# A selective scan laid out as four state groups over whole images, with its front spread behind it and a part of its products moved to POOL

## The chip, the cores and the metric

One core of a Trainium2 chip runs the whole network in one launch. The metric is the time of that launch on the device, in microseconds. Every kernel below ran at least four times on the same chip as the kernel before. The rounds ran on several chips; the median of the kernel before was 11377 to 11384 us on each, so runs of different rounds are compared here too. All the runs of one kernel agree within 0.3%.

## The reference

Four layers follow one another on a batch of 8 images. The first two hold a Mamba block: a norm, an input projection, a causal convolution with four taps, silu, a selective scan with 16 states for each of 768 channels, a gate and an output projection. Between and after them come an attention pooling, an MLP, two depthwise convolutions of 13 x 13 and a pointwise one. The change touches only the two Mamba blocks:

```python
u = silu(conv1d(xin))                       # 768 channels, 1024 tokens an image
dbc = u @ x_proj_w.T                        # step ranks, B and C
delta = softplus(dt_lo @ dt_proj_w.T + dt_proj_b)
def step(h, inp):
    dt_t, u_t, B_t, C_t = inp
    dA = exp(dt_t[..., None] * A)           # A: 768 x 16
    h = h * dA + (dt_t * u_t)[..., None] * B_t[:, None, :]
    y = einsum('bdn,bn->bd', h, C_t)
    return h, y
out = ((y + u * D) * silu(z)) @ out_proj_w.T
```

## The kernel before

Channels lie on the partitions, 6 chunks of 128. An image is two units of 512 tokens. For one chunk, ACT writes the decay (an exponential) into PSUM, POOL multiplies B by du, DVE scans and multiplies by C, and PE adds the 16 states up with an identity matrix. In the middle of a unit the next unit's front (norm, projection, convolution, silu) is issued.

```python
def softplus(s, d):
    ...                                                   # one product on PE into ps
    nc.scalar.activation(e, ps, AF.Abs, bias=dt_b[:, d : d + 1])
    nc.vector.tensor_scalar(delta, ps, dt_b[:, d : d + 1], 0.0, ALU.add, ALU.max)
    nc.scalar.activation(e, e, AF.Exp, scale=-1.0)
    nc.scalar.activation(r, e, AF.Identity, bias=k["one"])
    nc.scalar.activation(lw, e, AF.Ln, bias=k["one"])
    nc.vector.scalar_tensor_tensor(r, r, 1.0, e, ALU.subtract, ALU.subtract)
    nc.vector.tensor_tensor(lw, lw, r, ALU.subtract)
    nc.vector.tensor_tensor(delta, delta, lw, ALU.add)

def scan(s, d, y):
    delta = softplus(s, d)
    du = work.tile([P, T], F32, tag="du", name="du")
    nc.vector.tensor_tensor(du, delta, u, ALU.mult)
    for j in range(NS // 2):                              # two states at a time
        nc.gpsimd.tensor_tensor(dbu, s["Bt"][j], du.unsqueeze(1).to_broadcast([P, 2, T]), ALU.mult)
        for q in range(2):
            nc.scalar.activation(h[:, q], delta, AF.Exp, scale=A[:, n : n + 1])     # h in PSUM
        for q in range(2):
            nc.vector.tensor_tensor_scan(h[:, q], h[:, q], dbu[:, q], first, ALU.mult, ALU.add)
        if half == 0:
            nc.vector.tensor_copy(state[:, d, 2 * j : 2 * j + 2], h[:, :, T - 1])
        nc.vector.tensor_tensor(hc, h, s["Ct"][j], ALU.mult)
        for q in range(2):
            nc.tensor.matmul(acc, k["ident"], hc[:, q], ...)
    ...                                                   # y = (u * D + acc) * gate

for i in range(NU):
    gates(s, range(KD // 2))
    exp_ln()                                              # the table set of exp and ln
    for d in range(KD // 2):
        scan(s, d, y)
    gates(s, range(KD // 2, KD))
    nxt = front(i + 1) if i + 1 < NU else None
    exp_ln()
    for d in range(KD // 2, KD):
        scan(s, d, y)
    ...
```

In each queue the instructions stand in one order, which is fixed when the program is built. The building step puts the instructions in order by the dependencies, by the program order and by estimated durations.

## Time and profile before

| | before |
|---|---|
| time (median) | 11379 us |
| first layer, from the start to its last output | 4152 us |
| one image in the steady part of a layer | 515 us |
| of it DVE busy / idle | 450 / 62 us |
| from the start of the layer to its first scan | 77 and 63 us |
| stretches that the change does not touch | 3078 us |

DVE is the fullest engine of the layers, and its share falls below six tenths only outside them. Idle time is the sum of DVE's gaps over 0.15 us. I also use a third number below, "blocked": for each instruction of DVE, its duration above the tenth percentile of the instructions of the same line and shape, added up. It measures how long DVE stands inside an instruction without progress. In the kernel before it is 21 us an image.

### The profile page before, as it was taken

Reading aid. Unit: us, or ns where it says so; the run is one execution under the profiler, and the core shown is the slowest. Engines: PE = TensorE matmul, PEld = TensorE weight load, DVE = VectorE, ACT = ScalarE, POOL = GpSimd, SP = SyncE. Lnnn points to the kernel's source line nnn. Section 1 sums busy time; section 2 is a strip of 40 time slices with the busy share of each in tenths; the row PEclk is TensorE's granted clock in tenths of the full one; section 3 lists DMA queues with packets and bytes.
Section 4 is the critical chain, followed back from the end, with each engine's and each line's share of the span. In section 5 each row is a group of like instructions: output and inputs, shape, how many; then the busy total and the mean of one; then the engine's idle time right before and its main releaser. Section 6 shows DMA issues by size and latency. Waiting matters only on the chain. (4 is left out here: it accounts for less than half of the span.)

```text
span 11377.1 us, 62759 instructions
## 1 busy us (share of the span) xinstructions
PE 8400.4 (74%) x18924; PEld 3687.4 (32%) x18924; DVE 7542.9 (66%) x8579; ACT 4328.4 (38%) x6060; POOL 3877.4 (34%) x1750
## 2 busy tenths in 40 slices
PE   6676677767677665766767677666676888889999
PEld 2222222222222211222222222222222333358688
DVE  7888888888888863788888888888887111110100
ACT  4444444444444432444444444444443221210100
POOL 3444444444444430344444444444444000001011
PEclk8898989888888886889888988888888999989999
DMA  1111111111111100111111111111110101024444
GB/s 62 60 44 38 41 38 38 39 38 38 56 55 38 36 29 28 54 44 62 44 38 41 38 38 39 38 38 47 59 41 29 22 17 22 15 55 84 128 85 79
DMA packets 703234, 523.10 MB, mean 46 GB/s; under 512 B 553344, under 2 KB 566784, under 8 KB 701872
## 3 DMA queue, kind: packets, MB, share of 16 engines
q1 hardware_dynamic: 573616, 456.16, 13.7%
q10 hardware_dynamic: 120064, 37.76, 1.3%
q0 software_dynamic: 9216, 25.18, 1.0%
q8 instruction: 150, 2.46, 0.1%
q14 instruction: 188, 1.54, 0.0%
HBM read 438.81 MB, written 80.15 MB: 46 GB/s over the span
## 5 line engine op out<-in xcount | busy, mean ns | idle before, releaser
L218 POOL TENSOR_TENSOR dbu<-Bt,du 128x1024 f32<-128x1024 f32 x1536 | 3683.4, 2403 | 5037.6 <-DVE h L226 2493.6
L232 PE MATMUL acc<-hc,ident 128*128 128x512 f32 x6144 | 3476.6, 701 | 2045.0 <-DVE hc L230 2032.7
L222 ACT ACTIVATE h<-delta,A 128x512 f32<-128x512 f32 x3072 | 2095.6, 689 | 3074.2 <-DVE hc L230 3030.7
L232 PEld LDWEIGHTS acc<-hc,ident 128*128 128x128 f32 x6144 | 1236.2, 218 | 4260.8 <-DVE hc L230 3168.8
L226 DVE TENSOR_TENSOR_SCAN h<-h,state,dbu 128x512 f32<-128x512 f32 x1536 | 1920.7, 1276 | 108.5 <-POOL dbu L218 101.6
L226 DVE TENSOR_TENSOR_SCAN h<-h,dbu 128x512 f32<-128x512 f32 x1536 | 1842.1, 1218 | 114.7 <-POOL dbu L218 106.0
L230 DVE TENSOR_TENSOR hc<-h,Ct 128x1024 f32<-128x1024 f32 x1536 | 1854.5, 1211 | 14.7
L433 PE MATMUL ps<-xp,wt 128*128 128x256 f32 x4992 | 1100.2, 382 | 20.0 <-DMA wt<-k_cols 20.0
L433 PEld LDWEIGHTS ps<-xp,wt 128*128 128x128 f32 x4992 | 942.5, 189 | 178.0 <-issue 21.0
L370 DVE SCALAR_TENSOR_TENSOR x<-ps_fc,vecs,x 128x512 f32<-128x512 f32 x48 | 36.0, 750 | 1019.3 <-PE ps_fc L369 1019.3
L182 PE MATMUL ps_z<-xt,w_in 128*128 128x512 f32 x1152 | 617.0, 679 | 88.2 <-ACT zs L187 44.3
L246 PE MATMUL ps_out<-y,w_out 128*128 128x512 f32 x1152 | 596.2, 654 | 106.2 <-DVE y L236 67.7
L364 PE MATMUL ps_fc<-xt,fc 128*128 128x512 f32 x1152 | 533.9, 627 | 126.8 <-ACT xt L93 126.8
L428 POOL DMA_DIRECT2D xp<-x x192 | 169.8, 885 | 1302.6 <-PE ps L433 910.9
L135 PE MATMUL ps_in<-xt,w_in 128*128 128x512 f32 x1152 | 550.0, 619 | 47.8 <-ACT xt L93 47.8
L369 PE MATMUL ps_fc<-h,fc 128*128 128x512 f32 x1152 | 497.0, 592 | 0.0
L435 ACT ACTIVATE o<-ps,b_grp 128x256 f32<-128x256 f32 x192 | 91.1, 475 | 1002.8 <-PE ps L433 1002.8
L473 DVE TENSOR_TENSOR o<-o,xt 128x512 f32<-128x512 f32 x48 | 33.3, 693 | 655.2 <-ACT o L470 655.2
L152 DVE SCALAR_TENSOR_TENSOR u<-xp,vecs,u 128x512 f32<-128x512 f32 x576 | 422.0, 744 | 4.2
L85 ACT ACTIVATE sq<-xt 128x512 f32<-128x512 f32 x192 | 113.8, 624 | 807.7 <-DVE xt L81 759.4
L357 POOL COPY xt<-x 128x1536 f32<-128x1536 f32 x16 | 23.5, 1469 | 1133.4 <-PE ps_fc L364 1095.0
L182 PEld LDWEIGHTS ps_z<-xt,w_in 128*128 128x128 f32 x1152 | 237.7, 214 | 448.4 <-issue 298.7
(124 smaller groups left out, 6390.7 us busy)
## 6 DMA issues: line engine op xcount, KB each, us to landing
Bt<-bc SPq DMA_DIRECT2D x256, 512.0 KB, 4.3
Ct<-bc SPq DMA_DIRECT2D x256, 512.0 KB, 4.8
wt<-k_cols SPq DMA_DIRECT2D x768, 52.0 KB, 2.7
xt<-x SPq DMA_DIRECT2D x48, 768.0 KB, 5.1
x<-o SPq DMA_DIRECT2D x96, 256.0 KB, 2.0
xp<-x POOLq DMA_DIRECT2D x192, 128.0 KB, 4.3
xt<-in_x_dram SPq DMA_DIRECT2D x16, 768.0 KB, 4.4
o<-in_x_dram SPq DMA_DIRECT2D x48, 256.0 KB, 2.8
```

The lines of the kernel that those rows point to most:

```text
L135: nc.tensor.matmul(ps, w_in[:, c, d * P : (d + 1) * P], xt[:, c], start=c == 0, stop=c == KC - 1)
L152: nc.vector.scalar_tensor_tensor(u, xp[:, j : j + T], conv_w[:, 4 * d + j : 4 * d + j + 1], u, ALU.mult, ALU.add)
L182: nc.tensor.matmul(ps, w_in[:, c, DI + d * P : DI + (d + 1) * P], s["xt"][:, c], start=c == 0, stop=c == KC - 1)
L218: nc.gpsimd.tensor_tensor(dbu, s["Bt"][j], du.unsqueeze(1).to_broadcast([P, 2, T]), ALU.mult)
L222: nc.scalar.activation(h[:, q], delta, AF.Exp, scale=A[:, n : n + 1])
L226: nc.vector.tensor_tensor_scan(h[:, q], h[:, q], dbu[:, q], first, ALU.mult, ALU.add)
L230: nc.vector.tensor_tensor(hc, h, s["Ct"][j], ALU.mult)
L232: nc.tensor.matmul(acc, k["ident"], hc[:, q], start=j == 0 and q == 0, stop=j == NS // 2 - 1 and q == 1)
L246: nc.tensor.matmul(ps, w_out[:, d, m * P : (m + 1) * P], y[:, d], start=d == 0, stop=d == KD - 1)
L364: nc.tensor.matmul(ps, w1[:, c, m * P : (m + 1) * P], xt[:, c], start=c == 0, stop=c == KC - 1)
L369: nc.tensor.matmul(ps, w2[:, f, m * P : (m + 1) * P], h[:, f], start=f == 0, stop=f == KF - 1)
L433: nc.tensor.matmul(ps, wt[:, j], xp[:, :, j : j + HW], start=j == 0, stop=j == KS - 1)
```

## The change

The intent is to take load off DVE and to make its instructions longer. A block is 32 channels by four groups of states on the 128 partitions, so that one scan goes over 1024 tokens and no state is carried between halves. The sum over the four groups is a product with a 128x32 matrix that writes 32 rows of PSUM, a different group of the array's columns for each block. Of eight products with C, three go to POOL, with the scan writing SBUF for these. Silu runs in bursts of six, with an added order on ACT: all earlier activations first, then the burst, then the rest. The front of the next image and the output of the last are spread over the scan in 48 slots. Delta, du, u, z and y travel through memory to change their layout. The first tap of the convolution and the max in softplus go from DVE to ACT.

```diff
+POOL_C = (2, 5, 7)
...
-                u = work.tile([P, T], F32, tag="u", name="u", bufs=9)
-                nc.vector.tensor_scalar(
-                    u, xp[:, 0:T], conv_w[:, 4 * d : 4 * d + 1], conv_b[:, d : d + 1], ALU.mult, ALU.add
-                )
+                    nc.scalar.activation(
+                        u, xp[:, 0:T], AF.Identity, bias=conv_b[:, d : d + 1], scale=conv_w[:, 4 * d : 4 * d + 1]
+                    )
...
+                act.burst([(z, z, AF.Silu) for z in zs])
+                for d in range(KD):
+                    nc.sync.dma_start(s["uz"][d][:, 1, cols], zs[d])
+                yield
...
-            nc.vector.tensor_scalar(delta, ps, dt_b[:, d : d + 1], 0.0, ALU.add, ALU.max)
+            nc.scalar.activation(delta, ps, AF.Relu, bias=dt_b[:, d : d + 1])
...
+                for q in range(4):
+                    nc.sync.dma_start(t[32 * q : 32 * q + 32], s["dd"][d][32 * j : 32 * j + 32, i])
...
+                            w_ = work.tile([P, L], F32, tag="slab", name="slab", bufs=6)
+                            nc.gpsimd.tensor_tensor(w_, s["Bt"][n], du4, ALU.mult)
+                            h = ps_da.tile([P, L], F32, tag="h", name="h")
+                            nc.scalar.activation(h, dl, AF.Exp, scale=A[:, at : at + 1])
+                            if (2 * n + i) % 8 in POOL_C:
+                                nc.vector.tensor_tensor_scan(w_, h, w_, 0.0, ALU.mult, ALU.add)
+                                nc.gpsimd.tensor_tensor(w_, w_, s["Ct"][n], ALU.mult)
+                            else:
+                                nc.vector.tensor_tensor_scan(h, h, w_, 0.0, ALU.mult, ALU.add)
+                                nc.vector.tensor_tensor(w_, h, s["Ct"][n], ALU.mult)
+                            hs.append(w_)
+                        for half in range(2):
+                            for i in range(2):
+                                rows = slice(32 * (2 * jp + i), 32 * (2 * jp + i) + 32)
+                                nc.tensor.matmul(
+                                    acc[rows, half], k["sel"], hs[i][:, half * T : (half + 1) * T],
+                                    start=n == 0, stop=n == NL - 1,
+                                )
+                        pull()                            # one slot of the front behind
...
```

## The prediction

> **What bounds the kernel now.** I read the page first (busy shares, slices, costliest groups), then a table of stretches.
>
> ```profile
> PE 8400.4 (74%) x18924; PEld 3687.4 (32%) x18924; DVE 7542.9 (66%) x8579; ACT 4328.4 (38%) x6060; POOL 3877.4 (34%) x1750
> ...
> DVE  7888888888888863788888888888887111110100
> ACT  4444444444444432444444444444443221210100
> POOL 3444444444444430344444444444444000001011
> ...
> L218 POOL TENSOR_TENSOR dbu<-Bt,du 128x1024 f32<-128x1024 f32 x1536 | 3683.4, 2403 | 5037.6 <-DVE h L226 2493.6
> ...
> L226 DVE TENSOR_TENSOR_SCAN h<-h,state,dbu 128x512 f32<-128x512 f32 x1536 | 1920.7, 1276 | 108.5 <-POOL dbu L218 101.6
> L226 DVE TENSOR_TENSOR_SCAN h<-h,dbu 128x512 f32<-128x512 f32 x1536 | 1842.1, 1218 | 114.7 <-POOL dbu L218 106.0
> L230 DVE TENSOR_TENSOR hc<-h,Ct 128x1024 f32<-128x1024 f32 x1536 | 1854.5, 1211 | 14.7
> ```
>
> The two plateaus of DVE at 8 tenths are the two scan layers. PE has the largest share of the span, but much of it lies in the tail, where DVE is nearly empty. In the layers POOL is at 4 tenths and waits for DVE's scans, which barely wait for POOL (some 0.1 ms per row). Three rows, two forms of the scan and the product with C, hold 5617 us of DVE. The next view is three stretches: one steady image of the second layer (two units of 512 tokens), then the pooling between the layers and everything after the second layer.
>
> ```profile
> 5171.70:5689.00 517.30, 361.48 (x672) 132.07 (x672) 450.88 (x504) 240.82 (x333) 230.41 (x98) 0.88 0.13 42
> ...
> 4151.00:4594.00 443.00, 247.52 (x393) 80.52 (x393) 142.18 (x235) 108.99 (x168) 0.00 (x0) 0.69 0.11 38
> 8742.00:11377.00 2635.00, 2371.08 (x7780) 1493.58 (x7780) 192.41 (x277) 418.49 (x625) 193.35 (x208) 0.94 0.28 58
> ```
>
> After the length come PE, PEld, DVE, ACT and POOL busy. In an image DVE works 450.9 of 517.3 us and idles 66. The change does not touch the last two stretches: 443 + 2635 = 3078 us stay. The two layers are the other 8299 us, 4150 each, and the whole change has to earn its money there. The chain of waits is of no use: it names the depthwise convolutions, which merely come last.
>
> **The lock between DVE and POOL.** POOL is to get more work, so I asked what the two do to each other. Two neighbouring steps of softplus, both reading two SBUF tiles, and then the timeline around one late product:
>
> ```profile
> L206 DVE TENSOR_TENSOR sp_l<-sp_l,sp_r x192: 665/692/2227, 71.9 to 8649.7; 128x512 f32<-128x512 f32 x192
> ```
> ```profile
> L207 DVE TENSOR_TENSOR delta<-delta,sp_l x192: 666/674/694, 72.6 to 8667.8; 128x512 f32<-128x512 f32 x192
> ```
> ```profile
> 4013.49 2.35 POOL L218 TENSOR_TENSOR dbu<-Bt,du 128x1024 f32<-128x1024 f32 x1 [2.39 <-DVE h L226]
> ...
> 4015.03 1.36 DVE L236 TENSOR_TENSOR y<-y,zs 128x512 f32<-128x512 f32 x1
> ```
>
> Same shape, same engine: L206 goes up to 2227 ns, L207 never above 694. I matched each with POOL's products in the trace: 50 of the 192 L206 begin while POOL is running, with 1409 ns of it left, and take 1956 ns on average; the other 142 take 678. No L207 begins under a POOL product. In the timeline L236 begins at 4015.03, POOL ends at 4015.84, DVE at 4016.39: 0.81 us waiting, 0.55 us working. The scans (1166 begin under POOL, mean 1248 ns, against 1246 of the rest) are not touched; they read one tile from PSUM and one from SBUF.
>
> **What the Trainium skill says.** "SBUF — State Buffer", section "Who interferes with whom": a DVE instruction with two SBUF inputs and a GpSimd instruction that reads SBUF exclude one another for a whole instruction; with at most one SBUF input there is no contention. The figures above agree. "GPSIMD Engine Reference", section "Elementwise — side-by-side cycle accounting": a two-input product costs POOL about 2.6 cycles an element at 1.2 GHz, DVE about one at 0.96 GHz; for 1024 elements that is 2.2 us against 1.1 us, and the rows show 2.40 (2.35 undisturbed) and 1.21. So moving a product saves DVE 1.2 us and costs POOL 2.35. "ScalarE: Activation LUTs", section "What ACT_TABLE_LOAD costs": 1283 ns a load, the duration that this trace has for every load. "TensorEngine Tiling (Array Packing)", section "Key Properties": tiles can run in parallel; no run here shows it yet.
>
> **The change part by part, one image.** Elements to scan: 24 blocks x 4 states x 1024 = 98304 columns, as before (6 x 16 x 1024). Putting four state groups on the partitions therefore saves no scan work, only instruction starts and the state copies.
>
> Scan, 96 of 128x1024. A tensor_tensor takes 680 ns for 512 columns (L207) and 1211 for 1024 (L230): about 149 ns fixed. Taking the same off 1247 leaves 1098 ns per 512 columns, so 2 x 1098 + 149 = 2.345 us each; 225.1 us. Before: 192 x 1.247 = 239.4.
> Product with C: 96 x 1.211 = 116.3 before; 5 of 8 stay, 60 x 1.211 = 72.7. The other 36 go to POOL.
> Removed: state copies (48 x 0.15 = 7.2; they came in one half only, so 3.6 a unit), first tap of the convolution (12 x 0.537 = 6.4) and softplus's max (12 x 0.738 = 8.9), both to ACT.
> Kept front, by its rows without blocking: taps 36 x 0.744 = 26.8; softplus and du 48 x 0.68 = 32.6; norm 2 x 6 = 12; carries 3.
> Output: 12 x 0.737 + 6 x 1.21 = 16.1 for y; 6 x 0.75 = 4.5 for the residual.
> Sum 392.8 us of durations. Neighbours overlap: in the steady unit durations of 242 make 225 us of union over 264 instructions, 0.063 us each; with some 290 instructions that is 18. DVE works about 374 us an image, 77 less than now.
>
> POOL: 96 + 36 = 132 products x 2.35 = 310 us, from 230. In about 460 us it is 67% full before any blocking, from 45%.
>
> Lock: DVE instructions with two SBUF inputs are 36 taps, 48 of softplus and du, 6 of the norm and 6 for y: 96. Today few meet POOL (L207, du and the taps never do, in step with the scan). With the front spread behind the scan and POOL two thirds full I take 55% of them to meet it, with 1.3 us left (1.28 and 1.41 us in today's L205 and L206): 96 x 0.55 x 1.3 = 69 us. This is where I chose, and it is the largest uncertainty.
>
> Other idle time of DVE: today 66 us an image, mostly waiting for ACT in the norm and softplus, with no scan in the queue at that place. Scan work now stands between, and of the loads of tables only 8 an image remain, in four bursts of 6 x 0.63 + 2 x 1.28 = 6.3 us, which two exponentials ahead (some 7 us of scan and products) nearly hide. I leave 20 us.
>
> Image with a front behind it: 374 + 69 + 20 = 463 us, against 515.
>
> Beside it: ACT has 96 exponentials of about 1.15 us (the 8x1024 exponential of the pooling took 1147 ns) and perhaps 110 us of the rest, half the time. PE has as many instructions as now, 361 us. Transfers: dl and du4 24 x 1 MB, B and C 4 MB, u, z, y out and in and delta, du out 25 MB, x and the result 5 MB: 58 MB, 125 GB/s; the third slice from the end of today's page moves 128 GB/s with the DMA engines 4 tenths busy. Loads are issued two blocks ahead, some 35 us, where today's land in 2 to 5 us.
>
> Ends of a layer: the first scan starts at 76.9 us now, after half an image's front. A whole image, with gates, softplus and a trip through memory, is 170 us by estimate. The last image has no front behind it: 225 + 73 + 16 + 4.5 less overlap is 307, POOL 310; 330. Its output projection, halves in turn from memory, is 45.
> Layer: 170 + 7 x 463 + 330 + 45 = 3786, against 4150. Total 2 x 3786 + 3078 = 10650 us, 6.4% faster.
>
> **Rivals.** (1) The lock takes the gain. Consecutive taps may let POOL in between each, so that each waits a whole 2.35 us; at 0.9 x 1.8 x 96 = 156 us the image takes 550 and the total about 11900. L205's 1834 ns under POOL speaks for it; against it, POOL is then itself delayed and has idle time left, and a waiting tap works as soon as POOL ends. (2) POOL bounds the quiet stretches: two slots need 2.75 x 2.35 = 6.5 us of POOL, 6.1 of DVE. With only six slabs nothing averages over longer stretches. That costs 10 to 20 us an image, total 10900. (3) The queue of transfers or the fixed order on ACT starves the scan: some 310 issues an image at 0.4 us are 125 us, but a store whose data are late holds the loads behind it; 11200 if it happens at each step. (4) The lock costs little, because the order of the queues falls into step as it does today (25 us), and idling nearly vanishes: 410 an image, 9900.
>
> **Range and chances.** Between (4) and part of (1) to (3): 10050 to 11150, eight times in ten. Faster by over 2% (below 11151) 0.88; within 2% 0.08; slower 0.04.
>
> **What would show it.** Scan of 1024 columns at 2.3 to 2.4 us; DVE busy, waits within it included, 440 to 460 us an image; taps and softplus above 1.1 us in the mean, with maxima above 2.2 us; POOL near 70% in the layers; steady image 463 us; the stretches outside the layers unchanged. Wrong if the scan's row has kept 2.5 us, if DVE idles over 60 us an image on POOL, ACT or transfers, or if the two-input rows stay at 0.7 us (then the time is near 9700, the sum without the 69 us).

## The result and the profile after

The changed kernel takes 11953 us (median of 4, 11945 to 11954), the kernel before 11379. The ratio is 1.050 (95% interval 1.049 to 1.052): slower by 5%, where 6.4% faster was predicted. Ratios here are the mean time of one kernel's runs over that of the other's of the same rounds, so they are not quite the ratios of the medians.

The page of the changed kernel: busy shares, slices, and the groups that answer to those of before. After the bar stand busy us and mean ns, then the idle time of the engine before the group.

```profile
PE 7955.7 (67%) x18924; PEld 2948.1 (25%) x18924; DVE 7085.9 (59%) x5222; ACT 3809.7 (32%) x4718; POOL 5442.1 (46%) x2326
...
DVE  4878787777777773388777787877878110110000
...
POOL 2656565565655670066655565655668000001011
...
L271 POOL TENSOR_TENSOR slab<-Bt,du 128x1024 f32<-128x1024 f32 x1536 | 3819.1, 2513 | 2409.2 <-DMA dl<-dd 1005.2
L279 DVE TENSOR_TENSOR_SCAN h<-h,slab 128x1024 f32<-128x1024 f32 x960 | 2184.9, 2286 | 1252.0 <-ACT h L274 730.7
...
L277 POOL TENSOR_TENSOR slab<-slab,Ct 128x1024 f32<-128x1024 f32 x576 | 1450.5, 2518 | 1615.0 <-DVE slab L276 1467.5
...
L276 DVE TENSOR_TENSOR_SCAN slab<-h,slab 128x1024 f32<-128x1024 f32 x576 | 1310.1, 2274 | 19.9 <-ACT h L274 12.5
L280 DVE TENSOR_TENSOR slab<-h,Ct 128x1024 f32<-128x1024 f32 x960 | 1151.4, 1208 | 10.4 <-DVE h L279 0.5
...
L188 DVE SCALAR_TENSOR_TENSOR u<-xp,vecs,u 128x512 f32<-128x512 f32 x576 | 728.1, 1276 | 67.7 <-ACT u L184 67.7
```

DVE's work fell, from 7543 to 7086 us, and POOL's rose, from 3877 to 5442. In a steady image no engine is as full as DVE was (450 of 515 us; now DVE works 425 of 556). But the main scan now has 1252 us of idle time ahead of it, where the two rows of before had 223 between them, and a tap of the convolution (L188) went from 744 to 1276 ns though nothing in it was changed. The tap's row in the kernel before was:

```profile
L152 DVE SCALAR_TENSOR_TENSOR u<-xp,vecs,u 128x512 f32<-128x512 f32 x576 | 422.0, 744 | 4.2
```

A steady image of the changed kernel, then the two stretches that should not have moved (length, then busy PE, PEld, DVE, ACT, POOL):

```profile
2391.40:2947.30 555.90, 331.32 (x672) 85.32 (x672) 425.72 (x294) 201.21 (x243) 329.36 (x132) 0.75 0.37 107
...
4462.00:4905.00 443.00, 248.26 (x393) 80.91 (x394) 142.20 (x235) 109.52 (x168) 0.00 (x0) 0.69 0.11 38
9316.00:11951.00 2635.00, 2373.46 (x7780) 1494.27 (x7780) 192.38 (x277) 418.20 (x625) 193.10 (x208) 0.94 0.28 58
```

The untouched stretches are 3078 us again, to within 1 us. Everything happened in the two layers. From the times of the first scan of each image in both traces, the 574 us of profile span divide like this:

| | before | after | difference, both layers |
|---|---|---|---|
| start of a layer to its first scan | 77, 63 | 224, 211 | +295 |
| seven images of a layer, each | 516 | 546 | +423 |
| last image and the rest of the layer | 469, 469 | 402, 393 | -143 |

The last image is shorter because nothing of a front runs behind it. For DVE the sums below are means over the third to seventh image of the first layer, in us an image:

| | before | after |
|---|---|---|
| time | 515 | 556 |
| DVE busy | 450 | 425 |
| of it blocked | 21 | 64 |
| DVE idle | 62 | 129 |

So 68 us of work are gone (450 - 21 against 425 - 64), blocking took back 43 and idling 68, and the image is 41 us longer.

Where is the idle time? Four places recur in each image. First, twice an image, at the gates of the two halves (the timeline of the changed kernel; start, duration, and in brackets the idle time before it):

```profile
2492.93 1.12 ACT L274 ACTIVATE h<-dl,A 128x1024 f32<-128x1024 f32 x1 [0.87 <-DVE slab L276]
2504.36 2.23 ACT L96 ACTIVATE xt<-xt,vecs 128x512 f32<-128x512 f32 x3 [10.31 <-DVE xt L91]
2509.13 0.58 ACT L156 COPY z<-ps_z 128x512 f32<-128x512 f32 x1 [2.54 <-PE ps_z L149]
...
2523.90 3.23 ACT L404 ACTIVATE z<-z 128x512 f32<-128x512 f32 x6
2527.14 1.28 ACT L395 ACT_TABLE_LOAD   x1
2528.44 2.15 ACT L274 ACTIVATE h<-dl,A 128x1024 f32<-128x1024 f32 x2
...
2500.55 3.78 DVE L91 TENSOR_TENSOR xt<-xt,rs_y 128x1536 f32<-128x1536 f32 x1
2529.65 4.48 DVE L279 TENSOR_TENSOR_SCAN h<-h,slab 128x1024 f32<-128x1024 f32 x2 [25.33 <-ACT h L274]
```

ACT is idle most of the time between 2493 and 2524, but the next exponential of the scan stands behind the burst in its queue, the burst behind six copies of z, these behind the projection on PE and that behind the norm on DVE. The end of the norm, L91, itself takes 3.78 us, twice its usual 1.75, because it waits first for a product of POOL that ends at 2502.71. DVE then has nothing to scan for 25 us.

Second, at each start of an image (SPq is the queue that issues the loads):

```profile
2915.51 1.36 SPq L237 DMA_DIRECT2D Bt<-bc  x3
2925.97 0.34 SPq L296 DMA_DIRECT2D y<-uzt  x1
2926.41 2.14 SPq L237 DMA_DIRECT2D Bt<-bc  x4
2928.60 7.84 SPq L237 DMA_DIRECT2D Ct<-bc  x16
2936.73 1.88 SPq L248 DMA_DIRECT2D dl<-dd  x4
2938.84 1.91 SPq L248 DMA_DIRECT2D du<-dd  x4
...
2924.72 1.23 DVE L295 TENSOR_TENSOR uzt<-uzt 128x1024 f32<-128x1024 f32 x1
2947.35 2.30 DVE L279 TENSOR_TENSOR_SCAN h<-h,slab 128x1024 f32<-128x1024 f32 x1 [21.40 <-POOL slab L271]
```

The queue stands 9.0 us, from 2916.9, at the store of y (L296), because DVE finishes the last sum of the image (L295) only at 2925.95. The loads of B and C stand behind this store, although the last use of the old C ended at 2919.7; from the third image of a layer on, each starts with the same 9 us. Then a load starts every 0.5 us or so, and twenty of them are ten us before dl and du even start. Third, the output of the image before, whose 36 records stand in one piece in PE's queue, ahead of the sums of the scan:

```profile
2424.78 17.34 PE L309 MATMUL ps_out<-yt,w_out 128*128 128x512 f32 x36
...
2442.06 5.34 PE L285 MATMUL acc<-slab,sel 128*32 128x512 f32 x22
```

During these 17 us PE frees no slab (a buffer of a product). This first time it costs little: POOL then idles 1.9 us for a slab and DVE 2.2 us for POOL's product. The second half of the output, 17.03 us from 2452.66, costs more: DVE stands 4.4 us at the output itself and then 11.4 us at the sum that PE has not reached. Fourth, DVE's own collection of a finished sum waits at the head of DVE's queue, 32 us an image in six pieces, of which those 11.4 us are one.

The blocking is visible in the two-input instructions. These are rows of softplus in the changed kernel (minimum, median, maximum), to be held against L206 and L207 of the prediction:

```profile
L226 DVE TENSOR_TENSOR sp_l<-sp_l,sp_r x192: 656/679/2836, 87.7 to 8884.3; 128x512 f32<-128x512 f32 x192
```
```profile
L227 DVE TENSOR_TENSOR delta<-delta,sp_l x192: 658/668/2718, 88.4 to 8887.0; 128x512 f32<-128x512 f32 x192
```

The step that never met a POOL product before (694 ns at most) now goes up to 2718.

### The profile page after: what moved, and what is told of

Same layout as the page of the kernel before. It is cut to its first block, busy times and chain, and to the rows that moved or that the text cites. A ratio compares the mean times of both kernels' runs of the same rounds, so it can differ in the third digit from the quotient of the medians.

```text
span 11950.9 us, 65751 instructions
## 1 busy us (share of the span) xinstructions
PE 7955.7 (67%) x18924; PEld 2948.1 (25%) x18924; DVE 7085.9 (59%) x5222; ACT 3809.7 (32%) x4718; POOL 5442.1 (46%) x2326
## 4 chain that ended last, share of the span: by engine, by line
PE 29%; DVE 14%; issue 8%; POOL 6%; DMA 3%; ACT 3%; SPq 0%; DVEq 0%; POOLq 0%; ACTq 0%
PE ps L575 9%; PE ps_fc L506 4%; PE ps_fc L511 4%; POOL slab L271 4%; DVE h L279 4%; PE ps_z L149 2%; POOL slab L277 2%; PE ps_out L309 2%; DVE u L188 2%; PE acc L285 2%; DVE slab L276 2%; DVE slab L280 1%; PE var L89 1%; PE ps L611 1%; PE mean L83 1%
## 5 line engine op out<-in xcount | busy, mean ns | idle before, releaser
L285 PE MATMUL acc<-slab,sel 128*32 128x512 f32 x6144 | 2963.4, 851 | 3010.2 <-DVE slab L280 1715.6
L271 POOL TENSOR_TENSOR slab<-Bt,du 128x1024 f32<-128x1024 f32 x1536 | 3819.1, 2513 | 2409.2 <-DMA dl<-dd 1005.2
L279 DVE TENSOR_TENSOR_SCAN h<-h,slab 128x1024 f32<-128x1024 f32 x960 | 2184.9, 2286 | 1252.0 <-ACT h L274 730.7
L274 ACT ACTIVATE h<-dl,A 128x1024 f32<-128x1024 f32 x1536 | 1709.2, 1116 | 3478.5 <-DVE slab L280 1674.2
L277 POOL TENSOR_TENSOR slab<-slab,Ct 128x1024 f32<-128x1024 f32 x576 | 1450.5, 2518 | 1615.0 <-DVE slab L276 1467.5
L285 PEld LDWEIGHTS acc<-slab,sel 128*32 128x32 f32 x6144 | 478.4, 132 | 5377.9 <-POOL slab L277 1843.3
L276 DVE TENSOR_TENSOR_SCAN slab<-h,slab 128x1024 f32<-128x1024 f32 x576 | 1310.1, 2274 | 19.9 <-ACT h L274 12.5
L280 DVE TENSOR_TENSOR slab<-h,Ct 128x1024 f32<-128x1024 f32 x960 | 1151.4, 1208 | 10.4 <-DVE h L279 0.5
L188 DVE SCALAR_TENSOR_TENSOR u<-xp,vecs,u 128x512 f32<-128x512 f32 x576 | 728.1, 1276 | 67.7 <-ACT u L184 67.7
L309 PE MATMUL ps_out<-yt,w_out 128*128 128x512 f32 x1152 | 544.5, 632 | 25.1 <-DMA yt<-y 23.6
```

Of the source, the lines that this page charges most:

```text
L188: nc.vector.scalar_tensor_tensor(u, xp[:, j : j + T], conv_w[:, 4 * d + j : 4 * d + j + 1], u, ALU.mult, ALU.add)
L271: nc.gpsimd.tensor_tensor(w_, s["Bt"][n], du4, ALU.mult)
L274: nc.scalar.activation(h, dl, AF.Exp, scale=A[:, at : at + 1])
L276: nc.vector.tensor_tensor_scan(w_, h, w_, 0.0, ALU.mult, ALU.add)
L277: nc.gpsimd.tensor_tensor(w_, w_, s["Ct"][n], ALU.mult)
L279: nc.vector.tensor_tensor_scan(h, h, w_, 0.0, ALU.mult, ALU.add)
```

## The experiments

Two theories were to be told apart. "Order": the pace is set by instructions that wait at the head of an in-order queue while others behind them could run. "Lock": the pace is set by DVE and POOL excluding one another, that is, by the products moved to POOL. Later a third appeared, "work": waits only show where an engine's work binds, so that removing one makes another.

All runs in one table; time is the median, the ratio is to the kernel before, the other columns are as above (us an image, mean of five images of the first layer). The second layer differs from the first by up to 10 us an image in most of these kernels, and by more in e14 (502 against 485) and e16 (484 against 495); a difference of a few us in one layer alone is therefore weak evidence. The record's verdict, which needs 2%, is "same" for e8, e10, e11 and e12 and "unclear" for e9, but the intervals of all five exclude a ratio of 1.

| run | time | ratio | image | DVE busy | of it blocked | idle |
|---|---|---|---|---|---|---|
| before | 11379 | 1 | 515 | 450 | 21 | 62 |
| after | 11953 | 1.050 | 556 | 425 | 64 | 129 |
| e1_late | 11808 | 1.038 | 543 | 424 | 61 | 117 |
| e2_onedma | 11890 | 1.045 | 532 | 419 | 58 | 112 |
| e3_no_pool_c | 12060 | 1.060 | 564 | 458 | 55 | 105 |
| e4_taps_psum | 11791 | 1.036 | 542 | 410 | 48 | 131 |
| e5_no_order | 11856 | 1.042 | 546 | 431 | 67 | 112 |
| e7_evict | 11870 | 1.043 | 549 | 425 | 63 | 122 |
| e8_all | 11493 | 1.010 | 502 | 403 | 42 | 98 |
| e9_no_pool | 11159 | 0.980 | 493 | 406 | 3 | 85 |
| e6_before_pool_c | 12047 | 1.059 | 556 | 446 | 54 | 106 |
| e10_before_pool_c2 | 11443 | 1.005 | 519 | 433 | 44 | 83 |
| e11_before_act | 11513 | 1.011 | 524 | 440 | 24 | 80 |
| e12_before_both | 11480 | 1.009 | 522 | 427 | 52 | 90 |
| e13_before_ahead | 10876 | 0.956 | 485 | 455 | 29 | 27 |
| e14_ahead_pool_c | 11024 | 0.969 | 485 | 448 | 66 | 35 |
| e15_ahead_act | 10778 | 0.947 | 474 | 446 | 31 | 25 |
| e16_ahead_both | 10981 | 0.965 | 495 | 444 | 72 | 47 |

### Removing one wait from the changed kernel

**e1_late**, the gates' burst three slots later in program order:

```diff
-                act.burst([(z, z, AF.Silu) for z in zs])
-                for d in range(KD):
-                    nc.sync.dma_start(s["uz"][d][:, 1, cols], zs[d])
                 ...
                 for d in range(KD):                      # the convolution
+                    if d == 3:
+                        act.burst([(z, z, AF.Silu) for z in zs])
+                        ...                              # and the stores of z; one more buffer of u and z
```

> The gates' silu burst comes three slots later in program order. Theory 'order' (scan starves behind the fixed order on ACT): the two waits of some 25 us an image of the scan for its exponential vanish, an image falls from 551 to about 505 us, the total to about 11250. Theory 'lock' (DVE and POOL excluding each other set the pace): the waits shrink but the scan then runs into POOL; less than 200 us in all, above 11750.

The wait for the exponential fell from 53 to 11 us an image, but the image only from 556 to 543: DVE's wait for POOL's slabs rose from 35 to 45, softplus got 8 and the carry 4 of its own. That is 145 us in all. "Lock" was nearer in its number; what the time went to, though, was mostly new waits (blocking even fell by 4).

**e5_no_order**, the silus without the added order on ACT:

```diff
     def burst(self, todo):
+        for out, x, func in todo:
+            self.nc.scalar.activation(out, x, func)
+        return
         before = self.close()
```

> Silu activations without the added order on ACT; the schedule may put exponentials between them, with more loads of tables. Theory 'order': the 53 us an image of the scan waiting for its exponential fall below 20, ACT gains perhaps 50 us of table loads an image, which it has free; image 515 to 530, total 11400 to 11600. If ACT's loads then hold the scan instead: above 11900.

Near e1: the wait for exponentials fell to 27 us (20 in one scan's row and 6 in the other), ACT worked 264 us an image in place of 201 because of the table loads, and the image got 11 us shorter. The strict order on ACT is thus a cause of the long waits, but not the whole of the loss; my 11400 to 11600 was missed.

**e2_onedma**, one transfer of 128 partitions where there were four of 32:

```diff
-                for q in range(4):
-                    nc.sync.dma_start(t[32 * q : 32 * q + 32], s["dd"][d][32 * j : 32 * j + 32, i])
+                nc.sync.dma_start(t, s["dd"][d][32 * j : 32 * j + 32, i].unsqueeze(0).to_broadcast([4, 32, L]))
```

(and B and C likewise)

> B, C, dl and du4 each loaded by one transfer over 128 partitions in place of four over 32. Theory 'order': the wait of 22 us at each start of an image, which is 36 issues of 0.48 us one after the other, falls to about 8, and loads held up behind the output's get shorter: 15 to 25 us an image, total 11600 to 11750. Theory 'lock': no change beyond 100 us.

A steady image lost 25 us, as "order" said; DVE's wait for POOL's slabs fell from 35 to 3. The total fell by 63 us only. The trace shows where the rest went: the last image and what follows grew from 402 to 491 us, because the building step had now put the collection of a sum earlier in DVE's queue there, and DVE stood 15 us at it four times. One edit far away reordered another stretch.

**e7_evict**, the collection after the next chunk's first two scans in program order:

```diff
                             hs.append(w_)
+                        if acc is None:
+                            if last is not None:
+                                finish(s, *last)         # collects the chunk before
+                            acc = ps_y.tile([P, 2, T], F32, tag="acc", name="acc")
+                            ...                          # and the load of u and z for this chunk
```

> The changed kernel with the collection of a finished chunk's sum put after the first two scans of the next chunk in program order. Theory 'order': DVE's wait for the sum, 32 us an image, falls below 10 and an image to about 530, total about 11600. If the wait merely moves to POOL's slabs: above 11850.

A miss. The wait fell only from 32 to 28 us an image; program order did not change much in the order of the queue. The image is 8 us shorter in the first layer, but in the second it is unchanged (549.5 against 550.1). The run says that this was no good handle, not whether the wait matters.

**e4_taps_psum**, the three taps accumulate in PSUM, so that each reads only one SBUF tile:

```diff
-                        u, xp[:, 0:T], AF.Identity, ...
+                        ps, xp[:, 0:T], AF.Identity, ...
...
-                            u, xp[:, j : j + T], conv_w[:, 4 * d + j : 4 * d + j + 1], u, ALU.mult, ALU.add
+                            ps if j < 3 else u, xp[:, j : j + T], conv_w[:, 4 * d + j : 4 * d + j + 1], ps, ALU.mult, ALU.add
```

> The convolution's taps accumulate in PSUM, so that each reads one SBUF tile. Both theories: mean of a tap from 1276 ns to about 745. Theory 'lock': 19 to 23 us an image less, total 11600 to 11680. Theory 'order': the time won is waited away elsewhere, total above 11800.

The costliest groups of DVE in this kernel have the taps at their old speed:

```profile
L188 DVE SCALAR_TENSOR_TENSOR ps_in<-xp,vecs,ps_in 128x512 f32<-128x512 f32 x384 | 283.4, 740 | 77.9 <-ACT ps_in L184 77.1
...
L188 DVE SCALAR_TENSOR_TENSOR u<-xp,vecs,ps_in 128x512 f32<-128x512 f32 x192 | 139.8, 730 | 0.6
```

From 1276 ns to 740 and 730 with the same arithmetic: the second SBUF input is what made them wait. The taps did not escape POOL by their timing: 327 of the 576 still begin under a product of POOL, and these take 736 ns, the others 739. Blocking fell by 16 us an image, idle time stayed, and the image fell by 14.5. So the lock's cost does reach the time. 162 us of the total are less than "lock" asked for and a little more than "order" allowed; both theories hold a part.

**e3_no_pool_c**, all products with C on DVE:

```diff
-POOL_C = (2, 5, 7)
+POOL_C = ()
```

> All products with C on DVE. Theory 'lock': POOL 43 percent full in place of 60, the excess of DVE's two-input instructions falls from 65 us an image to below 40, and though DVE takes over 44 us of products the time does not rise, 11700 to 11950. Theory 'order': idle time stays near 129 us an image and the 44 us of products come on top, less some 10 for shorter ends of a chunk: 12200 to 12400.

In between again. DVE got 32 us more busy (44 of products, less 9 of blocking and some overlap), idled 25 less, and the image grew by 8. The three products on POOL, one of the main points of the change, are worth 8 us an image (4 in the second layer), and not the 44 that they take off DVE.

**e8_all**: e1, e2, e4 and e7 in one.

> Late gates' burst, one transfer per tile, taps in PSUM and late collection together. Theory 'order': idle time falls from 129 to about 50 us an image and blocking by 16, image about 465, total 10800 to 11000, faster than the kernel before. If the waits are one shared bound seen at several places, the gains do not add: above 11400.

The image fell by 54.6 us; the four single gains were 13.5, 24.8, 14.5 and 7.8, which is 60.6. In the second layer they add to 40 and the image fell by 52; in total time they add to 453 us and e8 gained 460. So the gains add, and the waits are not one bound seen at several places, although the total is above the 11400 that the expectation took as the sign of that: the gains themselves were smaller than it assumed. But 98 us of idle time remain, the start of a layer went from 224 to 250 us, the last image again suffers as in e2 (499), and the total, 11493, is still slower than the kernel before.

**e9_no_pool** takes POOL out of the scan altogether. Its result is wrong on purpose. (The comparison, within its tolerance, cannot see B.)

```diff
-POOL_C = (2, 5, 7)
+POOL_C = ()
...
-                            nc.gpsimd.tensor_tensor(w_, s["Bt"][n], du4, ALU.mult)
...
-                                nc.vector.tensor_tensor_scan(h, h, w_, 0.0, ALU.mult, ALU.add)
+                                nc.vector.tensor_tensor_scan(h, h, du4, 0.0, ALU.mult, ALU.add)
```

> Wrong result on purpose: no product on POOL at all; the scan takes du itself, and all products with C are on DVE. Theory 'lock': excess of two-input instructions from 64 (55 with C on DVE) to below 5 us an image. Theory 'order': the waits that do not name POOL (some 53 for ACT's exponential, 23 for the sum, 9 for the output, the start of an image) stay, so an image is 361 + 44 + 85 to 100 = 490 to 510 us, total 10950 to 11200. If POOL's pace, and not the order, made the idle time: image below 450, total below 10400.

One image (same columns as above):

```profile
2154.10:2648.30 494.20, 324.53 (x672) 84.66 (x672) 405.93 (x331) 200.89 (x242) 0.00 (x0) 0.76 0.42 120
```

Blocking is gone (3 us), so blocking comes from POOL's work. Against e3, which differs only in B's products, the image is 71 us shorter: 52 of blocking and 20 of idle time. But with no POOL at all DVE still idles 85 us an image, 32 of them for exponentials, 25 for sums, 20 for du at the start. "Order" had said 490 to 510 for an image; it is 493. The lock is a real cost of the layout, and it is not what makes most of the idle time.

### One part of the change on the kernel before

**e6_before_pool_c**, the moved products alone:

```diff
+                on_pool = j in (2, 5, 7)
+                hs = dbu if on_pool else h
...
-                    nc.vector.tensor_tensor_scan(h[:, q], h[:, q], dbu[:, q], first, ALU.mult, ALU.add)
+                    nc.vector.tensor_tensor_scan(hs[:, q], h[:, q], dbu[:, q], first, ALU.mult, ALU.add)
...
-                nc.vector.tensor_tensor(hc, h, s["Ct"][j], ALU.mult)
+                (nc.gpsimd if on_pool else nc.vector).tensor_tensor(hc, hs, s["Ct"][j], ALU.mult)
```

> The kernel before, with 3 of 8 products with C moved to POOL and nothing else. If DVE's work sets the pace there, 18 x 1.21 = 22 us a unit less on DVE, less some 6 of new blocking: 257.7 to about 242 us a unit, total about 10900. Theory 'lock': the blocking takes most of it, 11200 or more.

This one edit makes the old kernel 5.9% slower. It takes 36 x 1.21 = 44 us off DVE an image and gives back 32 of blocking and 45 of idling. A detail shows how the lock works. The state copies of two elements, which now read SBUF for three of eight:

```profile
L230 DVE COPY state<-h x480: 128/150/162, 84.0 to 9149.1; 128x2 f32<-128x2 f32 x160
L230 DVE COPY state<-dbu x288: 166/1510/2321, 93.1 to 9152.8; 128x2 f32<-128x2 f32 x144
```

A copy from PSUM takes 150 ns, the same copy from SBUF 1510 in the median.

**e10_before_pool_c2** repairs this (those copies on ACT, one buffer more for B's product):

```diff
-                dbu = work.tile([P, 2, T], F32, tag="dbu", name="dbu")
+                dbu = work.tile([P, 2, T], F32, tag="dbu", name="dbu", bufs=3)
...
-                    nc.vector.tensor_copy(state[:, d, 2 * j : 2 * j + 2], hs[:, :, T - 1])
+                    (nc.scalar.copy if on_pool else nc.vector.tensor_copy)(state[...], hs[:, :, T - 1])
```

> The kernel before with 3 of 8 products with C on POOL, one more buffer for B's product, and the copy of the state on ACT where it would be SBUF to SBUF on DVE. Theory 'lock': the copies' 19 us an image of blocking go, the rest stays; unit from 278.7 to 262 to 270 us, still no faster than before. If buffers were the cause of the loss: below 250 a unit, total below 11150.

259.5 us a unit, half of 519: better than expected, but no gain over the kernel before. DVE is 17 us less busy an image and idles 21 more. Buffers and copies together were a good part of e6's loss; which of the two is not separated.

**e11_before_act**, the first tap and the max on ACT:

```diff
-                nc.vector.tensor_scalar(
-                    u, xp[:, 0:T], conv_w[...], conv_b[...], ALU.mult, ALU.add
-                )
+                nc.scalar.activation(
+                    u, xp[:, 0:T], AF.Identity, bias=conv_b[...], scale=conv_w[...]
+                )
...
-            nc.vector.tensor_scalar(delta, ps, dt_b[:, d : d + 1], 0.0, ALU.add, ALU.max)
+            nc.scalar.activation(delta, ps, AF.Relu, bias=dt_b[:, d : d + 1])
```

> The kernel before with the first tap and the max of softplus on ACT and nothing else: 12 x 0.537 + 12 x 0.738 = 15 us of DVE an image less, and the wait of 21 us an image of that max for ACT partly gone. If DVE's work sets the pace: image 490 to 500, total 11000 to 11150. If the time is waited away: above 11300.

Slower by 1.1% with less work on the fullest engine. The view of waits, before and with the edit (us in total, times, longest):

```profile
DVE delta L201 <- ACT sp_e L200: 332.2, 48, 11.4
...
DVE sp_r L205 <- ACT sp_r L203: 129.2, 62, 3.7
```
```profile
DVE sp_r L205 <- ACT sp_r L203: 568.6, 62, 14.1
```

DVE waited for softplus's steps on ACT 461 us before and 569 with the edit: the chain on ACT got one instruction longer, and DVE waits for it with the scans standing behind in its queue. This is only a part: in the means of five images softplus's waits rose by 6 us, all idle time by 18; the rest is spread over several waits of 1 to 3 us. It was the hint for the last four runs.

**e12_before_both**, e10 and e11 together:

> The last two together. If gains add: e10's time less e11's gain. Theory 'lock': slower than e11 alone.

11480: no sum of gains, because there were none; a quarter of the loss of e11 was made good. "Lock" had asked for a time above e11's, and missed.

### Only the order

**e13_before_ahead** executes the arithmetic of the kernel before, with softplus and du of a chunk issued one chunk earlier in program order, and with a third buffer for delta and du, which that needs:

```diff
+        def ready(s, d):
+            delta = softplus(s, d)
+            du = work.tile([P, T], F32, tag="du", name="du", bufs=3)
+            nc.vector.tensor_tensor(du, delta, s["us"][d], ALU.mult)
+            s.setdefault("ready", {})[d] = delta, du
+
         def scan(s, d, y):
-            delta = softplus(s, d)
-            du = work.tile([P, T], F32, tag="du", name="du")
-            nc.vector.tensor_tensor(du, delta, u, ALU.mult)
+            delta, du = s["ready"][d]
...
             for d in range(KD // 2):
+                ready(s, d + 1)
                 scan(s, d, y)
...
             for d in range(KD // 2, KD):
+                if d + 1 < KD:
+                    ready(s, d + 1)
+                elif nxt is not None:
+                    ready(nxt, 0)
                 scan(s, d, y)
```

> The kernel before with softplus and du of a chunk put one chunk earlier in program order; no instruction more or less. Theory 'order' (waiting instructions at the head of an in-order queue set the pace): the 29 us an image that DVE waits for softplus's ACT steps fall below 8, image 488 to 495, total 10950 to 11070. Theory 'work' (the time is DVE's or POOL's work, and waits move elsewhere): total above 11300.

10876 us, 4.4% faster than the kernel before, with the same number of instructions on DVE, POOL and PE. (ACT has 166 more, all of them loads of tables, 736 in place of 570; so "no instruction more" was not quite met, and they did not undo the gain.) Over the whole run the two waits of the kernel before that stand at e11 fell from 461 to 274 us; the larger of them is now:

```profile
DVE delta L201 <- ACT sp_e L200: 216.6, 34, 7.2
```

Idle time fell from 62 to 27 us an image, more than the waits for softplus alone (those fell from 31 to 19, not below 8). DVE's wait for POOL's product fell from 13 us to nothing and that for the output projection from 12 to 2: with a chunk ready, these were covered too. Here "work" is refuted. No run has the third buffers without the new order, so the two are not separated.

**e14_ahead_pool_c**, **e15_ahead_act** and **e16_ahead_both** repeat the moved work on top of it:

> The same with 3 of 8 products with C on POOL, as in the run with one more buffer. If blocking eats the moved work here too: within 1 percent of e13. If it was softplus's wait that ate it: 2 percent or more faster than e13.

> e13 with the first tap and softplus's max on ACT. Theory 'order': with the chain taken ahead the 12 us an image of DVE work that this saves now show, 8 to 15 us an image, total 10700 to 10950. Theory 'work': as e11, slower than its base.

> e13 with both. Theory 'order' with the lock as measured: near e15, within 1 percent. Without a lock: 2 percent or more below e15.

One image each of e11, e13 and e15:

```profile
2171.10:2696.80 525.70, 366.98 (x673) 135.81 (x672) 440.35 (x481) 245.08 (x347) 228.34 (x98) 0.87 0.13 41
```
```profile
1998.00:2482.70 484.70, 347.91 (x673) 127.83 (x672) 455.21 (x506) 248.60 (x338) 234.48 (x96) 0.90 0.13 45
```
```profile
1965.10:2437.60 472.50, 352.84 (x672) 129.40 (x672) 446.15 (x481) 272.63 (x368) 233.59 (x96) 0.91 0.14 46
```

The same move of two small instructions to ACT cost 9 us an image before and gains 10 once the chain runs a chunk ahead (in the second layer 8 and 2): e15 takes 10778 us, 0.9% less than e13, 5.3% faster than the kernel before and the best here. The products on POOL bring nothing with it: e14 is 1.4% slower than e13 and e16 1.9% slower than e15, with 66 and 72 us an image of blocking. That was more against POOL than I had expected (within 1% each). But e14 and e16 also have three buffers for B's product in place of two and two for du in place of three; how much of their loss is the buffers' is not tested.

## Why the prediction was wrong

The prediction named as a sign of being wrong that DVE idles over 60 us an image on POOL, ACT or transfers, and that came true. Term by term, against the trace of the changed kernel:

**The work of DVE, 374 us an image: right, a little high.** DVE is busy 425 us, 64 of it blocked, which leaves 361. The scan was put at 2.345 us and takes 2.286 and 2.274; the product with C at 1.21 takes 1.208.

**The lock, 69 us an image: right in kind, and in size partly by luck.** 64 measured as blocking, though 21 of this kind exist in the kernel before too. The 96 two-input instructions that the prediction counted make 55 of the 64, and 7 come from one-input rows that it did not count. The signs came out as foretold, taps at 1276 ns in the mean and maxima above 2.2 us. What the prediction left out are one-input copies and scalar instructions from SBUF to SBUF; the carry of three elements went from 355 to 809 ns in the mean, the norm's tensor_scalar from a maximum of 428 to one of 2316. I had called this the largest uncertainty. It was not. Nor did rival (1), which gave 11900 and so came close to the result, come about as it was told: it asked for 156 us of lock. POOL was to be near 70% full in the layers; it works 329 of 556 us, 59%.

**"Other idle time of DVE": "I leave 20 us". This is the step that failed.** It is 129. Its three reasons each fell. "Scan work now stands between": it stands behind, in a queue that keeps its order. "Four bursts of 6.3 us, which two exponentials ahead nearly hide": the burst is short, but what stands ahead of it is not, and two exponentials ahead cover 7 of some 35 us. "Loads are issued two blocks ahead": not at the start of an image, where they stand 9 us behind the store of the last y and then behind each other. Rival (3) named both waits, a late store in the queue of transfers that holds the loads behind it and the fixed order on ACT, and made 11200 of them; I gave it little weight. With 109 us more an image, 14 images are 1526 us; the smaller busy time (425 in place of 374 + 69) takes 18 x 14 = 252 off; the images of the second layer and the first of each layer, which are shorter than the five that these means are of, account for the rest of what is measured, 14 x (546 - 463) = 1162 us.

**"170 us by estimate" to the first scan: 224 and 211.** 95 us for both layers. In the trace the two halves run one after the other, softplus of the first half ends at 109 us and of the second at 194, and the exponentials of the first scan again come behind the next image's gates (this costs some 6 us: the scan starts at 223.9, POOL's first product for it is done at 218.1).

**Last image and output, 375: 402 and 393**, 45 us in all. The three together are 1162 + 95 + 45 = 1302, and with the predicted 10650 this is 11952.

**Was it the order, or the lock?** Both, in these proportions: against the kernel before, blocking adds 43 us an image and idle time 68, while 68 of work are saved. e9 shows that idle time of 85 us exists without any POOL; e13 shows on the kernel before that the place of instructions in the queues, with the buffers needed for it, is worth 30 us an image with no change in the work of DVE, POOL and PE. Still open is how much of the changed kernel's 129 us could be had: single repairs gave 8 to 25 us each, e8 left 98, and I did not bring it below the time of the kernel before. Why e2 and e8 put the collection of the sums so badly in the last image, I can only lay to the building step; no run here tests it. The quiet and busy stretches of the plan (rival 2) were not separated either. Nor is the clock of PE: in a steady image the trace shows 0.75 of it granted, where it was 0.87 before, and no run tells how much of DVE's wait for the sums comes from that.

**What the skill said.** "SBUF — State Buffer", section "Who interferes with whom", carried the one term that came out right, and e4 and e9 agree with it: one SBUF input less, 536 ns less a tap; no POOL, no blocking. "TensorEngine Tiling (Array Packing)", section "Key Properties", says that different tiles can run in parallel; the timeline agrees: in the 5.34 us shown above, records of 0.59 us for two groups of columns start within 0.01 us of each other, and the next two 0.43 us later, which is the step from one full-width record to the next just before. It made no difference, because PE mostly waited for slabs.

## What to carry to other kernels

When an engine is 87% busy, look first at what its remaining 13% wait for: taking work off it gained nothing here until the chain that it waited for was issued one step ahead, and then the same move paid (0.9%). Work moved to POOL is not free for DVE even if POOL has room: here an instruction of DVE with two inputs in SBUF, or a copy from SBUF to SBUF, waited up to 2.2 us for a product of POOL that takes 2.35; count those instructions first, or give them a PSUM operand. Before spreading one stage behind another, follow the order of each engine's queue from the late stage's first wait back to what stands ahead of it; an added order on one engine turns every delay of the spread stage into a stop of the main one.

## What the Trainium skill lacked or had wrong

- "SBUF — State Buffer", section "Who interferes with whom", names copies among what contends, but gives no figure for a small one: a copy of two elements went from 150 ns to 1510 in the median (e6) when its source moved from PSUM to SBUF.
- "ScalarE: Activation LUTs", section "What ACT_TABLE_LOAD costs", adds a drain of about 1380 ns to each load of 1283. The loads here do take 1283 ns, but no such drain shows: in the changed kernel a copy ends at 53.15 us, the load runs from 53.17 to 54.45 and the next activation starts at 54.47. Of the 188 loads of this kernel, 144 have less than 0.1 us of idle time on either side.
- No page gives in time what one issue of a load costs on the SP queue of this chip (one has a count of cycles for earlier chips). Here one load of 128 KB over 32 partitions takes 0.42 us on the queue in the median, and the 28 issues of the timeline above (B, C, dl and du, from 2926.41 to 2940.75) are 14 us, 0.5 us each with the waits between them.
